# One-hot table rows on two engines, rows loaded on a second queue, states copied by ScalarE, and a gate in four pieces

## The chip, the core and the metric

One core of a Trainium2 chip runs the whole program. The metric is the device time of one execution in microseconds (us). The engines are named as in the profile: PE (TensorE, matrix products), PEld (its weight loads), DVE (VectorE), ACT (ScalarE), POOL (GpSimd) and SP (SyncE, which issues most DMAs).

## The reference

The input x has 8 batches of 512 tokens of 512 values. A layer norm gives xn, from which two branches are computed, and the result joins them:

```python
xn = layernorm(x)
s  = attention(xn)          # q, k silu'd and rotated; linear attention in chunks of 128 with decay;
                            # 16 heads of 32; gated by sigmoid(xn @ Wg1 @ Wg2); rmsnorm by head; @ Wo
g  = silu(mixture(xn))      # router: top 4 of 16 experts, softmaxed; each expert silu(x@wg)*(x@wu)@wd,
                            # plus a shared expert with a sigmoid gate
out = x + s * g
```

In a chunk the attention makes the scores k q times a decay mask, and a state (32 x 32 for each head) is carried from chunk to chunk: S_new = lam_C * S + k v.

## The kernel before

The program is one straight trace for a planner, which orders the instructions of DVE, ACT, POOL and SP by its own costs and due times; the order of PE is that of the trace (`on_pe`), and `behind(engine)` pins single instructions of other engines. The stages follow each other:

1. **First pass (0 to about 208 us).** For each batch b: `norm` (statistics on DVE, the root on POOL), `halves` (16-bit copies on POOL), `turn` (PE transposes), `route_1`, `route_2` (top 4) and `share_1`, `share_2` (shared expert). `load_x(b)` (L142 to L148) loads a batch into one of three buffers; a buffer is free when the transposes, the copies and the store of its old batch are done. These pieces are interleaved with the attention of batch 0, `sequence(0)`. Groups g of four heads go through `key`, `query` (`rotated`, L594: four projection steps on PE, Silu on ACT, then DVE's shuffle, two products and a sum), `by_token` (L618: transposes into bank "k", then kd on DVE), `scores` (L634) and `output` (L675).
2. **Sorting (about 208 to 250 us).** `sort` computes for each token and choice its place in a list of 143 blocks of 128 rows, by expert.
3. **Table (250 to 325 us), beside `sequence(1)`.** `table` (L463) turns the places into a list of tokens: for each 128 tokens it makes two one-hot matrices, `place` (128 wide, L497, then multiplied by the token's number, L499) and `block` (143 wide, L502), all f16 and from SBUF, and PE adds up place^T block (L516). 64 lists go in 8 groups of 16. The buffers stand in the room of the last `LATE` experts' weights, whose loads wait for the table's end. `table` is a generator: `between[0]()` takes one piece of it after each projection step on PE in `rotated` and `value`. A group is four pieces: `make` for the next group, then 5, 5 and 6 matmuls. `sequence(1)` has 8 projections of four steps, 32 pieces.
4. **Blocks (about 340 to 800 us).** For each of 143 blocks: a gather (POOL's queue), a DMA transpose of half of the row (SP's queue), PE transposes of the other half (`transpose_x`), copies on ACT (`join`), `gate_up` (L1042), Silu on ACT (L1046), `transpose_h`, `down`. `gate_3(FIRST)`, the Sigmoid gate of batch 2, stands behind the gate_up of block 2.
5. **The remaining attention (about 800 us to the end).** `sequence(b)` for b = 2 to 7, with the mixture's gathers and sums (`mixture`, `last`) on POOL, DVE and ACT beside it.

PSUM banks have tags: four "a", one "k", one "m", two "d". The four score banks ps (L654), the table's pn (L512), the gate's p2 (L585) and the blocks' transposes all take "a" in turn. In `scores`, DVE reads the states' products straight from bank "k" (L657, L659), makes qd (L664), and then reads the four score banks (L670); `by_token` of the next group writes bank "k" again. `sequence` calls `gate_3(b)` after the first key when batch b has no gate yet, which is so for b = 1.

Of the kernel before, what the change touches and what calls it, by code (L numbers as in the profile page):

```python
# [10 lines left out]
F32 = mybir.dt.float32  # L11
# [8 lines left out]
P = 128  # L20
# [74 lines left out]
def tile_block(ctx: ExitStack, tc: tile.TileContext, a: dict, out: bass.AP):  # L95
# [8 lines left out]
    def bank(tag, name):  # L104
        return pp.tile([P, 512], F32, tag=tag, name=name, bufs={"a": 4, "k": 1, "m": 1, "d": 2}[tag])
# [34 lines left out]

    xs_of = {}

    def load_x(b):
        t = p1.tile([P, NC, D], F32, tag="x", name=f"x_{b}", bufs=3)
        rows = x[b].rearrange("(t p) d -> p t d", p=P)
        for ts in [slice(i, i + 1) for i in range(NC)] if b == 0 else [slice(0, NC)]:
            nc.sync.dma_start(t[:, ts, :], rows[:, ts, :])
        xs_of[b] = t  # L148

    load_x(0)  # L150
    ident = load(const, "ident", [P, P])
    rt_w = load(p1, "rt_w", [P, KC, Q])
    fold = load(p1, "fold", [P, EA])
    load_x(1)
# [308 lines left out]
    def table(room):  # L463

        acc = room[:, :NB]
        free = [2 * NB + 2]
        half = room.bitcast(F16)
        quads = GROUP // QUAD  # L470

        def part(*shape):
            n = int(np.prod(shape))
            free[0] += n
            flat = half[:, free[0] - n : free[0]]
            return flat.rearrange("p (q j) -> p q j", j=QUAD) if len(shape) == 2 else (
                flat.rearrange("p (u q j) -> p u q j", u=quads, j=QUAD))

        count = part(NB, QUAD)
        nc.scalar.copy(count, whole.unsqueeze(2).to_broadcast([P, NB, QUAD]))  # L480
        homes = [(part(quads, P, QUAD), part(quads, NB, QUAD)) for _ in range(2)]

        def rows(of, n):
            return of.rearrange("p (u j) -> p u j", j=QUAD).unsqueeze(2).to_broadcast(
                [P, of.shape[-1] // QUAD, n, QUAD])

        def make(i):
            place, block = homes[i // GROUP % 2]
            for u in range(0, quads, 2):
                us = slice(u, u + 2)  # L490
                lists = slice(i + u * QUAD, i + (u + 2) * QUAD)
                first = lists.start % NT

                def counts(n):
                    return count[:, :n].unsqueeze(1).to_broadcast([P, 2, n, QUAD])

                nc.vector.tensor_tensor(  # L497
                    place[:, us], counts(P), rows(sp[:, 0, lists], P), ALU.is_equal)
                nc.vector.tensor_tensor(  # L499
                    place[:, us], place[:, us], rows(token[:, first : first + 2 * QUAD], P),  # L500
                    ALU.mult)
                nc.vector.tensor_tensor(  # L502
                    block[:, us], counts(NB), rows(sp[:, 1, lists], NB), ALU.is_equal)

        make(0)
        yield
        for i in range(0, TOPK * NT, GROUP):
            if i + GROUP < TOPK * NT:
                make(i + GROUP)
            yield  # L510
            place, block = homes[i // GROUP % 2]
            pn = bank("a", f"pn_{i}")  # L512
            for some in ((0, 5), (5, 10), (10, GROUP)):
                with on_pe():
                    for j in range(*some):
                        nc.tensor.matmul(  # L516
                            pn[:, :NB], lhsT=place[:, j // QUAD, :, j % QUAD],
                            rhs=block[:, j // QUAD, :, j % QUAD], start=(j == 0),
                            stop=(j == GROUP - 1))
                if some[1] == GROUP:  # L520
                    if i:
                        nc.vector.tensor_tensor(acc, acc, pn[:, :NB], ALU.add)
                    else:
                        nc.vector.tensor_copy(acc, pn[:, :NB])
                yield
        t = const.tile([P, NB], I32, tag="slot", name="slot")
        nc.vector.tensor_scalar(t, acc, float(B * N // 2), None, ALU.add)
        slots.append(t)
# [4 lines left out]
    def home(b):  # L533
        return other[0] if other and (b - FIRST) % 2 else att
# [44 lines left out]
        g1_of[b] = att.tile([P, N], F32, tag="tmp", name=f"g2_{b}", bufs=TMP)  # L579
        nc.scalar.copy(g1_of[b], pf)  # L580

    def gate_3(b):
        on_of[b] = home(b).tile([P, G, N], F32, tag="on", name=f"on_{b}", bufs=1)
        g1 = g1_of.pop(b)
        p2s = [bank("a", f"p2_{b}_{g}") for g in range(G)]  # L585
        with on_pe():
            for g in range(G):
                gq = slice(g * Q, (g + 1) * Q)
                nc.tensor.matmul(
                    p2s[g], lhsT=wg2[gq, :], rhs=g1[gq, :], start=True, stop=True)  # L590
        for g in range(G):
            nc.scalar.activation(on_of[b][:, g, :], p2s[g], AF.Sigmoid)

    def rotated(b, g, n, w):  # L594
        ps = bank("m" if n == "k" else "d", f"p{n}_{b}_{g}")
# [38 lines left out]
    def scores(b, g):  # L634
# [19 lines left out]
                    nc.tensor.matmul(  # L654
                        pss[j][:, cs], lhsT=kT[hs, cs], rhs=qT[hs, cs], start=True, stop=True)
        st = scr[0].tile([P, NC - 1, HD], F32, tag="state", name=f"state_{b}_{g}")
        nc.vector.tensor_copy(st[:, 0], pkv[:, :HD])  # L657
        for c in range(1, NC - 1):
            nc.vector.scalar_tensor_tensor(  # L659
                st[:, c], st[:, c - 1], lamc[:, g : g + 1], pkv[:, c * HD : (c + 1) * HD],  # L660
                ALU.mult, ALU.add)
        st_of[g] = st
        qd = scr[0].tile([P, NC - 1, C], F32, tag="qd", name=f"qd_{b}_{g}")
        nc.vector.tensor_tensor(  # L664
            qd, qT[:, C:].rearrange("p (c t) -> p c t", t=C),
            dq[:, g].unsqueeze(1).to_broadcast([P, NC - 1, C]), ALU.mult)
        qd_of[g] = qd
# [239 lines left out]
    def first():  # L907

        for b in range(B):
            route_1(b)  # L910
            yield
            share_1(b)
            yield
            if b + 2 < B:
                norm(b + 2)
            if b + 1 < B:
                halves(b + 1)
                turn(b + 1)
                xs_of.pop(b + 1)
                if b + 4 < B:  # L920
                    load_x(b + 4)
                yield
            route_2(b)
            yield
            share_2(b)
            yield
        next(sorting)
# [4 lines left out]
    norm(1)  # L932
    halves(0)
    xs_of.pop(0)
    load_x(3)
    pieces = first()
    for _ in range(5):
        next(pieces)
# [26 lines left out]
        tc.tile_pool(name="exps", bufs=1, side="right", reuse_waits="tile"))  # L965
    wexp = exps.tile([P, EA - 1, WE], F32, tag="wexp", name="wexp")
    wflat = wexp.rearrange("p e w -> p (e w)")
    LATE = 4
    for e in range(E - LATE):
        nc.sync.dma_start(wexp[:, e, :], a["experts"][:, e, :])  # L970
    filling = table(wflat[:, (E - LATE) * WE :])
# [117 lines left out]
    for i in range(NB + 2):  # L1089
        turn_rows(i + 2)  # L1090
        join(i + 1)
        gate_up(i)
        if i == 2:
            gate_3(FIRST)
        transpose_x(i + 2)
        transpose_h(i - 1)
        down(i - 2)
        gather(i + 4)
# [162 lines left out]
```

## Time and profile before

| | us |
|---|---|
| median of 11 runs | 1228.71 (1224.1 to 1233.45) |
| profiled execution | 1230.39 |
| its span | 1228.6 |
| PE busy in the span | 1177.2 (96%) |
| DVE busy | 767.4 (62%) |
| ACT busy | 407.0 (33%) |
| POOL busy | 448.1 (36%) |

The profile shows one execution. "Busy" counts the time of compute instructions; an instruction on DVE, ACT or POOL that waits inside for a port is counted as busy. In a timeline row stand the start, the duration, the engine, the line, the operation, out <- in with shape and number, and in brackets the idle time before it on its engine with what ended it. Neighbouring rows of one engine can overlap by some 0.1 us, so the step from start to start is shorter than the duration.

### The profile page before, as it was taken

How to read it: one execution, taken by the hardware profiler on the slowest of the kernel's cores; microseconds unless marked ns; L12 is line 12 of the kernel's file. 1: busy time of each engine (PE TensorE's matmuls, PEld its weight loads, DVE VectorE, ACT ScalarE, POOL GpSimd, SP SyncE). 2: the span in 40 equal slices, each digit the busy share in tenths (PEclk: the TensorE clock that was granted, in tenths of full speed). 3: DMA queues.
4: the chain of work that ended last, by engine and by line, in shares of the span. 5: the costliest groups of instructions: out<-in, count | busy, mean ns of one | idle time of the engine just before them, and what ended most of it. 6: DMA issues, size and time to landing. Idle time of an engine off the chain costs nothing. (4 is left out here: it accounts for less than half of the span.)

```text
span 1228.6 us, 21563 instructions
## 1 busy us (share of the span) xinstructions
PE 1177.2 (96%) x7799; PEld 698.4 (57%) x7799; DVE 767.4 (62%) x1652; ACT 407.0 (33%) x782; POOL 448.1 (36%) x430
## 2 busy tenths in 40 slices
PE   6998999989999999999999999999999999999997
PEld 3444554446467777777777776544554544445453
DVE  6378554899224444344444444887969789698784
ACT  3343333320254444444443443123141321411420
POOL 3222102100213333333333331580886857848211
PEclk9998999999999999999999999999999999999999
DMA  9784331181459999899998997950845636535011
GB/s 322 259 287 163 117 137 70 26 321 40 170 138 224 233 229 222 224 229 229 228 230 217 228 227 190 327 167 13 284 141 170 214 104 221 167 112 149 24 36 68
DMA packets 167719, 219.77 MB, mean 179 GB/s; under 512 B 93696, under 2 KB 102656, under 8 KB 165696
## 3 DMA queue, kind: packets, MB, share of 16 engines
q1 hardware_dynamic: 145936, 146.17, 40.1%
q0 software_dynamic: 21680, 72.23, 21.0%
q8 instruction: 64, 1.05, 0.4%
q14 instruction: 39, 0.32, 0.1%
HBM read 127.25 MB, written 72.35 MB: 162 GB/s over the span
## 5 line engine op out<-in xcount | busy, mean ns | idle before, releaser
L1042 PE MATMUL pgu<-wexp,xt 128*128 x1144 | 271.5, 381 | 2.6 <-ACT xt L1023 2.4
L1042 PEld LDWEIGHTS pgu<-wexp,xt 128*128 128x128 f32 x1144 | 217.3, 191 | 94.4 <-issue 31.4
L1001 POOL DMA_INDIRECT xg<-xn_d,slot x83 | 78.7, 948 | 284.2 <-DVE y L1072 168.2
L1047 DVE TENSOR_TENSOR slb<-slb,pgu 128x128 f32<-128x128 f32 x143 | 41.2, 288 | 206.1 <-ACT slb L1046 206.1
L1121 POOL DMA_INDIRECT yg<-y_d,posi x128 | 142.3, 1112 | 50.3 <-DMA m<-sh_d 22.7
L1025 ACT COPY xt<-pl 128x512 uint16<-128x512 uint16 x143 | 109.7, 767 | 149.2 <-DMA pl<-xg 91.5
L1063 PE MATMUL py<-wexp,hT 128*128 x286 | 147.3, 597 | 0.0
L556 PE MATMUL pv<-wv,xT 128*128 128x512 f32 x256 | 121.0, 611 | 4.3 <-DVE sh L370 2.6
L598 PE MATMUL pk<-xT,wk 128*128 128x512 f32 x256 | 120.9, 612 | 0.0
L598 PE MATMUL pq<-xT,wq 128*128 128x512 f32 x256 | 115.9, 593 | 0.0
L731 PE MATMUL pw<-wo,on 128*128 128x512 f32 x224 | 100.9, 596 | 1.5 <-ACT so L904 0.7
L1001 POOL DMA_INDIRECT more<-xn_d,slot x60 | 56.7, 945 | 114.4 <-DVE y L1072 113.5
L1153 POOL TENSOR_TENSOR xo<-xo,m 128x512 f32<-128x512 f32 x30 | 43.8, 1460 | 146.9 <-DVE m L1149 138.6
L1072 DVE TENSOR_SCALAR y<-py,xg 128x512 f32<-128x512 f32 x83 | 62.2, 750 | 30.2 <-PE py L1063 30.2
L556 PEld LDWEIGHTS pv<-wv,xT 128*128 128x128 f32 x256 | 46.5, 193 | 60.9 <-issue 55.2
L670 DVE TENSOR_TENSOR sc<-ps,dmask 128x512 f32<-128x512 f32 x128 | 79.4, 683 | 1.0 <-PE ps L654 1.0
L598 PEld LDWEIGHTS pq<-xT,wq 128*128 128x128 f32 x256 | 47.4, 191 | 52.1 <-issue 50.9
L598 PEld LDWEIGHTS pk<-xT,wk 128*128 128x128 f32 x256 | 46.7, 193 | 49.4 <-issue 47.1
L1046 ACT ACTIVATE slb<-pgu 128x128 f32<-128x128 f32 x143 | 39.7, 278 | 95.8 <-PE pgu L1042 95.2
L731 PEld LDWEIGHTS pw<-wo,on 128*128 128x128 f32 x224 | 41.3, 190 | 51.3 <-issue 44.7
L603 ACT ACTIVATE sk<-pk 128x512 f32<-128x512 f32 x32 | 19.1, 596 | 117.5 <-PE pk L598 102.1
L1072 DVE TENSOR_SCALAR y<-py,more 128x512 f32<-128x512 f32 x60 | 45.0, 750 | 20.6 <-PE py L1063 20.6
(166 smaller groups left out, 1749.5 us busy)
## 6 DMA issues: line engine op xcount, KB each, us to landing
y_d<-y SPq DMA_DIRECT2D x143, 256.0 KB, 2.9
wexp<-in_experts SPq DMA_DIRECT2D x16, 768.0 KB, 10.8
sh_d<-sh SPq DMA_DIRECT2D x32, 256.0 KB, 2.6
m<-sh_d SPq DMA_DIRECT2D x32, 256.0 KB, 4.1
xo<-in_x SPq DMA_DIRECT2D x32, 256.0 KB, 3.7
out<-xo SPq DMA_DIRECT2D x32, 256.0 KB, 2.3
x<-in_x SPq DMA_DIRECT2D x7, 1024.0 KB, 7.1
xT_d<-xT SPq DMA_DIRECT2D x7, 1024.0 KB, 5.1
```

The source lines that it names most:

```text
L556: nc.tensor.matmul(pv, lhsT=xT_of[b][:, k, t * P : (t + 1) * P], rhs=wv[:, k, :], start=(k == 0), stop=(k == KC - 1))
L598: nc.tensor.matmul(ps, lhsT=w[:, k, g * P : (g + 1) * P], rhs=xT_of[b][:, k, :], start=(k == 0), stop=(k == KC - 1))
L670: nc.vector.tensor_tensor(s, pss[j].rearrange("p (c t) -> p c t", t=C), dmask[:, g * HG + j].unsqueeze(1).to_broadcast([P, NC, C]), ALU.mult)
L731: nc.tensor.matmul(pw, lhsT=on_of[b][:, g, t * P : (t + 1) * P], rhs=wo[:, g, :], start=(g == 0), stop=(g == G - 1))
L1001: nc.gpsimd.indirect_dma_start(out=row(i), out_offset=None, in_=xn_d, in_offset=bass.IndirectOffsetOnAxis(ap=slot[:, i : i + 1], axis=0))
L1025: nc.scalar.copy(xt[:, KP:, :].bitcast(U16).rearrange("p k (t h) -> p h k t", h=2), turned(i).rearrange("p (h k) t -> p h k t", h=2))
L1042: nc.tensor.matmul(pg[:, : 2 * F], lhsT=xt[:, k, :], rhs=wflat[:, bass.ds(off + k * 2 * F, 2 * F)], start=(k == 0), stop=(k == KC - 1))
L1047: nc.vector.tensor_tensor(sl, sl, pg[:, F : 2 * F], ALU.mult)
L1063: nc.tensor.matmul(py, lhsT=hT_of.pop(i), rhs=wflat[:, bass.ds(off_of.pop(i) + KC * 2 * F, D)], start=True, stop=True)
L1072: gone.append(nc.vector.tensor_scalar(y, py, row(i).bitcast(F32)[:, bass.ds(at, 1)], None, ALU.mult).ins)
L1121: nc.gpsimd.indirect_dma_start(out=yg, out_offset=None, in_=y_d, in_offset=bass.IndirectOffsetOnAxis(ap=posi[:, r, g : g + 1], axis=0))
L1153: nc.gpsimd.tensor_tensor(xo, xo, m, ALU.add)
```

## The change

- `load_x` takes a queue. Batches 3 to 7 are loaded on POOL's queue, not SP's. `ident` is loaded between the first and the second piece of x_0.
- `table` has three pairs of buffers in place of two, so that it takes the room of five late experts (`LATE = 5`). The multiplication by the token's number runs on POOL. Groups 0 and 1 are made at the start, then five pieces are empty; after that a piece is 5, 5 or 6 matmuls, and `make` for the group after the next stands ahead of the first of the three.
- In `scores`, ACT copies all three states' products from bank "k" into SBUF, and DVE's two steps read them there. The first copy on DVE (L657) is gone. For b < 2, qd is made on POOL.
- `gate_3` takes a list of groups. For batch 2 its four groups stand behind gate_up of blocks 2, 3, 4 and 5, one in each.

```diff
-    def load_x(b):
+    def load_x(b, queue=nc.sync):
...
-            nc.sync.dma_start(t[:, ts, :], rows[:, ts, :])
+            queue.dma_start(t[:, ts, :], rows[:, ts, :])
+            if b == 0 and ts.start == 0:
+                xs_of["ident"] = load(const, "ident", [P, P])
...
-    ident = load(const, "ident", [P, P])
+    ident = xs_of.pop("ident")
...
-        homes = [(part(quads, P, QUAD), part(quads, NB, QUAD)) for _ in range(2)]
+        homes = [(part(quads, P, QUAD), part(quads, NB, QUAD)) for _ in range(3)]
...
-            place, block = homes[i // GROUP % 2]
+            place, block = homes[i // GROUP % 3]
...
-                nc.vector.tensor_tensor(
+                nc.gpsimd.tensor_tensor(
                     place[:, us], place[:, us], rows(token[:, first : first + 2 * QUAD], P),
                     ALU.mult)
...
         make(0)
-        yield
+        make(GROUP)
+        for _ in range(KC + 1):
+            yield
         for i in range(0, TOPK * NT, GROUP):
-            if i + GROUP < TOPK * NT:
-                make(i + GROUP)
-            yield
-            place, block = homes[i // GROUP % 2]
+            if i + 2 * GROUP < TOPK * NT:
+                make(i + 2 * GROUP)
+            place, block = homes[i // GROUP % 3]
...
-    def gate_3(b):
-        on_of[b] = home(b).tile([P, G, N], F32, tag="on", name=f"on_{b}", bufs=1)
-        g1 = g1_of.pop(b)
-        p2s = [bank("a", f"p2_{b}_{g}") for g in range(G)]
+    def gate_3(b, groups=range(G)):
+        if 0 in groups:
+            on_of[b] = home(b).tile([P, G, N], F32, tag="on", name=f"on_{b}", bufs=1)
+        g1 = g1_of[b]
+        p2s = {g: bank("a", f"p2_{b}_{g}") for g in groups}
...
-        nc.vector.tensor_copy(st[:, 0], pkv[:, :HD])
+        nc.scalar.copy(st.rearrange("p c e -> p (c e)"), pkv[:, : (NC - 1) * HD])
         for c in range(1, NC - 1):
             nc.vector.scalar_tensor_tensor(
-                st[:, c], st[:, c - 1], lamc[:, g : g + 1], pkv[:, c * HD : (c + 1) * HD],
-                ALU.mult, ALU.add)
+                st[:, c], st[:, c - 1], lamc[:, g : g + 1], st[:, c], ALU.mult, ALU.add)
...
-        nc.vector.tensor_tensor(
+        (nc.gpsimd if b < FIRST else nc.vector).tensor_tensor(
             qd, qT[:, C:].rearrange("p (c t) -> p c t", t=C),
             dq[:, g].unsqueeze(1).to_broadcast([P, NC - 1, C]), ALU.mult)
...
-                    load_x(b + 4)
+                    load_x(b + 4, nc.gpsimd)
...
-    load_x(3)
+    load_x(3, nc.gpsimd)
...
-    LATE = 4
+    LATE = 5
...
-        if i == 2:
-            gate_3(FIRST)
+        if 2 <= i < 2 + G:
+            gate_3(FIRST, [i - 2])
```

More of the change, by code (lines that the diff above doesn't have):

```diff
@@ L580, in gate_2 @@
         nc.scalar.copy(g1_of[b], pf)
-    def gate_3(b):
-        on_of[b] = home(b).tile([P, G, N], F32, tag="on", name=f"on_{b}", bufs=1)
-        g1 = g1_of.pop(b)
-        p2s = [bank("a", f"p2_{b}_{g}") for g in range(G)]
+    def gate_3(b, groups=range(G)):
[3 more added lines that the diff above has]
+        p2s = {g: bank("a", f"p2_{b}_{g}") for g in groups}
         with on_pe():
-            for g in range(G):
+            for g in groups:
                 gq = slice(g * Q, (g + 1) * Q)
@@ L590, in gate_3 @@
                     p2s[g], lhsT=wg2[gq, :], rhs=g1[gq, :], start=True, stop=True)
-        for g in range(G):
+        for g in groups:
             nc.scalar.activation(on_of[b][:, g, :], p2s[g], AF.Sigmoid)
+        if G - 1 in groups:
+            g1_of.pop(b)
     def rotated(b, g, n, w):
```

## The prediction

> **What bounds the kernel now.** I read the page's shares first, then the waits with TensorE (PE) as the waiting engine, then the stretches by time, then the timeline around the longest waits. The chain view names only the closing addition (L1159), so it says nothing of the middle. The page:
>
> ```profile
> PE 1177.2 (96%) x7799; PEld 698.4 (57%) x7799; DVE 767.4 (62%) x1652; ACT 407.0 (33%) x782; POOL 448.1 (36%) x430
> ```
>
> PE is idle for only 51.4 of 1228.6 us, so a change that takes no PE work away can gain only from idle pieces that it removes. About 19 us of them lie at the two ends (10.3 in the first 30 us, 8.6 in the last 29). The waits that this change aims at:
>
> ```profile
> PE pn L516 <- DVE sc L670: 6.4, 3, 4.3
> PE pk L625 <- DVE state L659: 4.1, 4, 1.6
> PE pt L1016 <- ACT on L592: 1.9, 1, 1.9
> ```
>
> Columns: us in total, times, longest. Together 12.4 us, plus some clock loss behind the longest. The stretches of the table (core time, then PE, PEld, DVE, ACT, POOL busy, granted clock):
>
> ```profile
> 250.00:270.00 20.00, 15.73 (x111) 8.31 (x110) 18.02 (x34) 5.51 (x9) 0.00 (x0) 0.91 0.96 364
> 270.00:300.00 30.00, 27.38 (x318) 17.82 (x317) 29.25 (x59) 3.67 (x5) 0.00 (x0) 1.00 0.33 127
> ```
>
> VectorE (DVE) is 90 and 98% busy, GpSimd (POOL) idle, and the clock is 0.91 around the 4.27 us stall: here DVE sets PE's pace. The timeline shows how:
>
> ```profile
> 250.89 0.69 DVE L497 TENSOR_TENSOR wexp<-wexp,sp 128x1024 f16<-128x1024 f16 x1 [1.04 <-ACT wexp L480]
> ...
> 257.51 2.48 DVE L670 TENSOR_TENSOR sc<-ps,dmask 128x512 f32<-128x512 f32 x4
> 258.25 0.82 PE L516 MATMUL pn<-wexp 128*128 128x143 f16 x5 [4.27 <-DVE sc L670]
> ```
>
> From 250.89 DVE builds one-hot rows; only at 257.51 does it read the four score banks (tag "a") that PE needs again.
>
> **Table: the multiplication moves to POOL.** Sixteen L499 instructions leave DVE, each 0.60 us from start to start: 9.6 us of DVE. What they cost on POOL, no row shows. The nearest are additions of 512 f32 on POOL, and a 16-bit copy:
>
> ```profile
> L1127 POOL TENSOR_TENSOR yg<-yg,yg 128x512 f32<-128x512 f32 x32 | 41.4, 1293 | 1.4 <-DMA yg<-y_d,posi 0.9
> L381 POOL TENSOR_TENSOR wr<-oh,w 128x512 f32<-128x512 f32 x3 | 5.1, 1686 | 0.2
> L266 POOL COPY hs<-x 128x512 uint16<-128x512 uint16 x32 | 21.6, 715 | 18.0 <-DMA xn_d<-hs 18.0
> ```
>
> An undisturbed L381 with a broadcast operand took 1.37 us. The new one has 1024 elements. By bytes it is 1.27 us (as a 512 f32 addition), by elements 2 x 1.37 = 2.75. The 16-bit copy spends 0.61 us undisturbed on 512 elements, about 1.2 ns each, which doesn't look like two elements at a time; so I lean to elements, less one fixed part of about 0.2 (the 128x4 L249 takes 0.23): 2 x 1.3 - 0.2 = 2.4 us. (By the Trainium skill, "GPSIMD Engine Reference", Elementwise — side-by-side cycle accounting, a two-input operation costs some 2.6 cycles of 1.2 GHz per element, an estimate of 2.2 us and a start for 1024; no row here shows it for f16.)
>
> What decides is what POOL does to DVE meanwhile. Later in the same trace both work:
>
> ```profile
> 865.12 2.16 DVE L1149 TENSOR_TENSOR m<-m,s 128x512 f32<-128x512 f32 x1
> ...
> 877.38 2.14 DVE L607 TENSOR_TENSOR qT<-sq,cos 128x512 f32<-128x512 f32 x1
> 877.69 1.27 POOL L1127 TENSOR_TENSOR yg<-yg,yg 128x512 f32<-128x512 f32 x1
> ```
>
> A DVE operation with both inputs in SBUF takes 0.68 us alone, but 2.14 here: it ends 0.56 us after POOL's addition does. A POOL addition at 874.64 that met a running DVE operation took 1.64 instead of 1.27, so they take turns. DVE operations that read PSUM (L692, L670) keep 0.68 and 0.62 under POOL. These rows are f32; the new pairs are f16. (The Trainium skill, "SBUF — State Buffer", Who interferes with whom, states an exclusive lock for a DVE operation with two SBUF inputs against a GpSimd one that reads SBUF, with no exception by type; it speaks against this change: by it the sum below stands, without it the table gains 6 us as in rival two. That no run here shows f16 is why I keep both.)
>
> So I count one shared way to SBUF. Before the last multiplication DVE needs it for 16 place rows x 0.60, 16 block rows x 0.66 and 12 rotation steps (L607 to L609 of two keys and two queries) x 0.60 = 27.4 us; POOL for 16 x 2.4 = 38.4, three qd (moved to POOL for b < 2; 384 elements, about 1.0 each) and 16 gaps of 0.15: 43.8. Sum 71.2 us, from 250.9 to 322.1. Of PE's order there then remains: half of the last group and a projection step 2.2, output(1,3), gate_1 and squares 5.0 (before: 313.54 to 318.50), value(2,3) 3.5. That puts L719 at 332.8; before it began at 324.23: **+8.6 us**.
>
> The other bound is PE's own path. All of make(0) and make(16) now stand before the attention's DVE work: 8 operations, 5.0 us, with three multiplications of 2.4 between them, and the state steps, which now read only SBUF, behind the fourth: scores are read from about 265.7, first bank free at 266.3. PE, done with key(1,2) at about 255.6, waits there at gate_3(1), some 10.7 us. Before, gate_3 began at 263.56 with 2.6 us of pn work behind it, that is like 261.0, so PE is 5.3 us later, less the other two L516 waits (0.95 + 1.21): +3.1. The later bound holds. I take **+9**, for some idle between turns. Ends: at 2.75 us each the port sum grows by 5.6 (+14); at 1.27 it ends at 304 and doesn't bind, and PE's path gives 266.3 - 4 x 1.13 = 261.8, that is +0.8 - 2.2 = -1.4. POOL's queue there holds nothing else than qd; output(1,g) on PE waits for that.
>
> **Gate spread over blocks 2 to 5.** The rows:
>
> ```profile
> 348.33 1.14 PE L589 MATMUL p<-g,wg 32*128 32x512 f32 x8
> ...
> 349.38 1.28 ACT L592 ACT_TABLE_LOAD   x1
> 350.68 2.06 ACT L592 ACTIVATE on<-p 128x512 f32<-128x512 f32 x4
> 351.33 0.69 PE L1016 MATMUL pt<-ident,more 128*128 128x128 f32 x2 [1.85 <-ACT on L592]
> ```
>
> Eight matmul instructions end in 1.14 us, as long as two take alone (L578, 1.13): four row groups run at once. Spread, each goes alone, 2 x 0.436 (L731: 24 in 10.46) = 0.87, four 3.5 us, so PE gains 2.4 us of work. And Silu (L1046) stands between the Sigmoids, with its own 1.28 us load at 353.02: eight loads for two. ACT per block: 0.28 + 0.77 + 0.37 for the block and 2 x 1.28 + 0.55 = 4.5 us, against a block of 2.92 (gate_up starts 360.08 and 363.00) + 0.87 = 3.8. Short by 0.7 x 4 = 2.9, less a lead of about 1.7 (ACT's idle before L1046): 1.2 of stall. Sum 3.5 + 1.2 against 1.14 + 1.85: **+1.7**. Ends: lead hides all, +0.5 (0 if a slow block behind the old stall, 0.46, goes too); hides nothing, +3.4. (The Trainium skill, "ScalarE: Activation LUTs", What ACT_TABLE_LOAD costs, adds a drain of 1.38 us to each switch, which would make it some 8 us more; here the Sigmoid starts 1.30 us after its load does, so the row decides.)
>
> **State by ACT.** The copy frees bank "k" before DVE's chain, so up to 4.1 us of L625 waits go. The new wait: the copy is queued on ACT behind the mixture's Silu, which waited 72.7 us in 19 pieces (longest 8.6) for DVE; by_token on PE waits for it, with one projection (3.5 us) as cover. DVE loses 32 copies of 0.18, but its steps now take turns with POOL. Between -4.1 and +5 (one wait of 8.6 past its cover); nearer the first, as ACT is only a third busy: **-2**.
>
> **No net time.** Loads of x on POOL's queue: five issues of about 1 us (L1121, 1.1; SP's took 0.4), waiting for turn(b+1); behind each stands the next rstd, before which POOL was idle 5.7 us or more from 57 us on. One such load costs DVE a wait of 1.62 us at 108.75, and with it part of a 3.37 us PE wait at 113.83: between -1.6 and +2. ident one issue earlier frees PE at 5.9 instead of 6.44, but PE then waits for sw at 13.55 all the same, and sw keeps its place: 0 to -0.5. Four qd on POOL in sequence(0): cover is its idle time. One expert more after the table: 768 KB, about 3 us at 235 GB/s, beside projections that need none of it; +2 if the first gathers wait.
>
> **Sum.** 9 + 1.7 - 2 = +8.7 us. The profiled execution took 1230.39 (span 1228.6 and 1.8 around it), 1.7 above the median 1228.71 of 11 runs; against its own time that is 1239.1, on the median's footing 1237.4; I forecast 1237.
>
> **Rivals.** Likeliest (0.6): one port, elements; 1231 to 1249. Rival one (0.15): POOL handles f16 by bytes; -1.4 + 1.7 - 2 = -1.7, 1227. For it: f16 doubles DVE's rate (1024 in 0.69); against it: the 16-bit copy. Rival two (0.2), on the other side: f16 one-hot rows on DVE don't take turns with POOL, whatever POOL takes up to 3 us. Then DVE's 5.0 us of makes stand alone, the first bank is free at 256.8, PE is 4.2 earlier than 261.0, and 2.2 of later waits go: -6.4 + 1.7 - 2 = -6.7, 1222. It decides once place and block keep 0.69 beside L499. Against it: every f32 pair seen. Rival three (0.05): ACT's queue blocks the state copies as well, +5 more than -2: above 1244, up to 1255.
>
> **Numbers.** 0.3% (3.7 us) is about what a measurement of this kernel can tell from no change: 1225.0 to 1232.4. Faster: rival two and part of rival one, 0.23. Same: the rest of it and the lower edge of the first, 0.14. Slower: 0.63. Range 1221 to 1249; the likeliest case's own is 1231 to 1249.
>
> **What would show it.** Right: L499 on POOL at 2.2 to 2.8 us; L497 and L502 with means well above 0.75; a PE wait at L589 or L516 of several us before 270; L719 after 330; nine L592 and L1046 table loads in place of three around 343 to 365; L625 waits under 1 us. Wrong: L497 at 0.69 beside POOL, L589 of group 1 by 258, L719 before 322.

## The result, and the profile after

The changed kernel takes 1259.11 us (median of 8 runs, 1255.64 to 1263.72), the kernel before beside it 1227.66: ratio 1.0254, 95% interval 1.0236 to 1.0272, so 31 us slower. Forecast were 1237 us and a range up to 1249: the sign was right, the size was not. The profiled execution took 1256.39 us, with a span of 1254.6.

I cut both spans at the same events: the copy of the count tile by ACT, the first pb matmul behind the table, the first Silu of an expert block, the last one, and the span's end.

| stretch | before, us | after, us | difference |
|---|---|---|---|
| start to count copy | 249.9 | 250.9 | +1.0 |
| count copy to pb (the table's stage) | 74.3 | 94.5 | +20.2 |
| pb to first block | 20.5 | 19.3 | -1.2 |
| first to last block | 420.7 | 416.8 | -3.9 |
| last block to the square roots of sequences 2 and 3 | 66.9 + 75.7 | 71.7 + 78.7 | +7.8 |
| from there to the end | 320.6 | 322.7 | +2.1 |

The two executions profiled differ by 26.0 us, the medians by 31.5. The blocks' -3.9 us says little: over the twenty profiles of this document that stretch took 416.1 to 423.1 us, and 416.9 to 420.1 in kernels whose table is as fast as before. Start with the page's shares: PE's busy time grew by 9.2 us for the same 7799 matmuls; a slower clock is in that.

```profile
PE 1186.4 (95%) x7799; PEld 703.6 (56%) x7799; DVE 786.3 (63%) x1596; ACT 424.0 (34%) x820; POOL 498.7 (40%) x459
```

The stretches of the table's stage (core time; PE, PEld, DVE, ACT, POOL busy; granted clock):

```profile
250.00:270.00 20.00, 8.72 (x74) 4.76 (x73) 18.92 (x21) 3.71 (x6) 13.73 (x6) 0.78 0.90 349
270.00:300.00 30.00, 26.36 (x199) 16.43 (x195) 21.99 (x34) 5.11 (x8) 12.52 (x6) 0.80 0.18 75
300.00:330.00 30.00, 24.58 (x299) 16.25 (x298) 22.66 (x38) 2.25 (x5) 14.23 (x7) 0.94 0.18 63
```

Before, the clock was 0.91, then 1.00 and 1.00. Over the whole stage, from the count copy to pb, PE was busy for 65.4 us before and 73.4 after; what these 8.0 us are follows below. The waits of PE over the whole span, in total, times, longest:

```profile
PE p L593 <- DVE sc L675: 11.3, 1, 11.3
...
PE pw L736 <- DVE m L1154: 5.4, 4, 1.8
PE pg L572 <- DVE sc L675: 4.4, 2, 2.4
PE ps L660 <- DVE sc L675: 4.4, 2, 3.6
...
PE pn L519 <- DVE sc L675: 3.5, 1, 3.5
```

Inside the table's stage PE waits 20.9 us in all, against 8.7 before: +12.2. Three waits are long, all for VectorE's reading of scores. The timeline of VectorE and GpSimd shows why the first is:

```profile
251.88 0.69 DVE L499 TENSOR_TENSOR wexp<-wexp,sp 128x1024 f16<-128x1024 f16 x1 [1.05 <-ACT wexp L482]
252.50 0.75 DVE L504 TENSOR_TENSOR wexp<-wexp,sp 128x1144 f16<-128x1144 f16 x1
253.16 2.38 DVE L499 TENSOR_TENSOR wexp<-wexp,sp 128x1024 f16<-128x1024 f16 x1
...
267.58 2.47 DVE L675 TENSOR_TENSOR sc<-ps,dmask 128x512 f32<-128x512 f32 x4
```

```profile
252.66 2.33 POOL L501 TENSOR_TENSOR wexp<-wexp,token 128x1024 f16<-128x1024 f16 x1 [18.85 <-DVE wexp L499]
255.62 2.34 POOL L501 TENSOR_TENSOR wexp<-wexp,token 128x1024 f16<-128x1024 f16 x1 [0.63 <-DVE wexp L499]
...
267.74 1.89 POOL L501 TENSOR_TENSOR wexp<-wexp,token 128x1024 f16<-128x1024 f16 x1 [0.63 <-DVE wexp L499]
```

The comparison that starts at 253.16 beside a multiplication lasts 2.38 us instead of 0.69, and ends 0.55 us after it: f16 operations take turns like the f32 ones of the trace before. The Trainium skill, "SBUF — State Buffer", Who interferes with whom, says so without exception by type; the row agrees. GpSimd waits too: the multiplication at 252.66 starts while the block row of 252.50 runs and lasts 2.33 us; the one at 267.74 meets only reads of score banks, which lie in PSUM, and lasts 1.89. Its own work is 1.9 us. What a long wait does behind itself, on PE:

```profile
268.31 3.86 PE L593 MATMUL p<-g,wg 32*128 32x512 f32 x8 [11.28 <-DVE sc L675]
...
286.74 2.07 PE L660 MATMUL ps<-qT,kT 32*128 32x128 f32 x8 [3.63 <-DVE sc L675]
288.75 2.08 PE L604 MATMUL pk<-xT,wk 128*128 128x512 f32 x2
...
293.30 1.04 PE L604 MATMUL pk<-xT,wk 128*128 128x512 f32 x2
...
312.00 0.82 PE L519 MATMUL pn<-wexp 128*128 128x143 f16 x5 [3.51 <-DVE sc L675]
312.64 1.97 PE L559 MATMUL pv<-wv,xT 128*128 128x512 f32 x2
```

A pair of projection matmuls takes 2.08 us right behind a wait and 1.04 some 5 us later: each of these waits is paid a second time. The gate's 3.86 us (1.14 at 348.33 of the trace before) is only in part the clock: its matmuls start at 268.31, 268.91, 269.51 and 270.11, as VectorE frees one score bank after the other. The rows that ran slow behind the three waits (the pairs of 1.91, 2.08, 1.42, 1.97 and 1.47 instead of 1.04, the ps row of 2.07 instead of 1.15, and smaller ones) add up to some 6 us by my count, against 1.4 before. So of the 8.0 us more of busy time, some 4.5 are the clock; the rest is matmuls that start bank by bank.

### The profile page after: what moved, and what is told of

It is laid out like the page before. It is cut to its first block, busy times and chain, and to the rows that moved or that the text cites. A ratio compares the mean times of both kernels' runs of the same rounds, so it can differ in the third digit from the quotient of the medians.

```text
span 1254.6 us, 21638 instructions
## 1 busy us (share of the span) xinstructions
PE 1186.4 (95%) x7799; PEld 703.6 (56%) x7799; DVE 786.3 (63%) x1596; ACT 424.0 (34%) x820; POOL 498.7 (40%) x459
## 5 line engine op out<-in xcount | busy, mean ns | idle before, releaser
L501 POOL TENSOR_TENSOR wexp<-wexp,token 128x1024 f16<-128x1024 f16 x16 | 36.7, 2295 | 48.3 <-DVE wexp L499 47.6
```

## The experiments

They ran on several chips; the kernel before took 1245.3, 1245.4, 1228.2, 1227.7 and 1241.2 us beside them. So all are told by the ratio to the kernel before on the same chip; 0.1% is 1.2 us. "Step" is the time from the count copy to the first pb matmul, from the profile.

### The parts one by one

Five kernels each put one part into the kernel before. First the multiplication alone:

```
-                nc.vector.tensor_tensor(
+                nc.gpsimd.tensor_tensor(
                     place[:, us], place[:, us], rows(token[...], P), ALU.mult)
```

> The kernel before with that one line moved to GpSimd. Turns at one way to SBUF: L497's mean goes above 1.1 us, L499 takes 2.2 to 2.4 on GpSimd, and the time is 10 to 25 us above before (1238 to 1253). If the layout of the pieces makes the loss: within 4 us of 1228.

Ratio 1.0087 [1.0057, 1.0117], step 86.9 us. The groups (busy, mean ns, idle before):

```profile
L499 POOL TENSOR_TENSOR wexp<-wexp,token 128x1024 f16<-128x1024 f16 x16 | 35.4, 2215 | 63.9 <-DVE wexp L497 63.9
L497 DVE TENSOR_TENSOR wexp<-wexp,sp 128x1024 f16<-128x1024 f16 x16 | 21.4, 1336 | 3.6 <-PE pn L516 2.5 <-ACT wexp L480 1.0
```

VectorE lost 16 instructions of 0.69 us, and its comparisons for `place` became nearly twice as long. Then the table's new layout with the multiplication on VectorE: three homes, rows two groups ahead, the start five pieces later, no piece for making alone, LATE 5.

```
         make(0)
-        yield
+        make(GROUP)
+        for _ in range(KC + 1):
+            yield
         for i in range(0, TOPK * NT, GROUP):
-            if i + GROUP < TOPK * NT:
-                make(i + GROUP)
-            yield
+            if i + 2 * GROUP < TOPK * NT:
+                make(i + 2 * GROUP)
```

> The kernel before with the table's new layout alone: three buffers, groups 0 and 1 made at the start, two groups ahead, LATE = 5, and the multiplication still on VectorE. If the order costs by itself (the scores' reads queue behind both groups, and gate_3 of batch 1, which needs all four banks, meets that wait), the table's stage is some 7 us longer than before (74.3 us) and the time is 5 to 9 us above before. If GpSimd makes the whole loss and the earlier end of the table is a gain, the time is 0 to 5 us below before.

Ratio 1.0077 [1.0046, 1.0107], step 82.9 us. Nothing in it touches GpSimd, so the new layout was no gain but a loss of its own. The state copied by ACT, alone:

```
-        nc.vector.tensor_copy(st[:, 0], pkv[:, :HD])
+        nc.scalar.copy(st.rearrange("p c e -> p (c e)"), pkv[:, : (NC - 1) * HD])
...
-                st[:, c], st[:, c - 1], lamc[:, g : g + 1], pkv[:, c * HD : (c + 1) * HD],
-                ALU.mult, ALU.add)
+                st[:, c], st[:, c - 1], lamc[:, g : g + 1], st[:, c], ALU.mult, ALU.add)
```

> The kernel before with the states copied by ScalarE, nothing else. The prediction's own value is 2 us below before (the L625 waits of 4.1 us go). The rival from the trace after: the wait only moves from the transposes to the next matmul that needs a score bank, and L659's second SBUF input doubles its mean (0.245 to about 0.5 us), so 0 to 6 us above before.

Ratio 1.0029 [1.0007, 1.0051]. The steps on VectorE now have two inputs in SBUF, and take turns with GpSimd. In the sequence of batch 3, first this kernel, then the one with the gate spread (states as before, same chip):

```profile
891.96 2.27 DVE L659 SCALAR_TENSOR_TENSOR state<-state,lamc 128x32 f32<-128x32 f32 x2
894.89 1.06 PE L569 MATMUL pg<-xT,wg 128*32 128x512 f32 x8 [1.92 <-DVE sc L669]
```

```profile
893.61 0.53 DVE L662 SCALAR_TENSOR_TENSOR state<-state,lamc,pk 128x32 f32<-128x32 f32 x2
894.93 1.06 PE L569 MATMUL pg<-xT,wg 128*32 128x512 f32 x8
```

The two steps take 2.27 us instead of 0.53, the scores behind them are read later, and PE waits. Between the square roots of batches 2 and 3 this kernel takes 80.3 us, the other 76.4. The gate spread, alone:

```
-        if i == 2:
-            gate_3(FIRST)
+        if 2 <= i < 2 + G:
+            gate_3(FIRST, [i - 2])
```

> The kernel before with the gate of batch 2 spread over blocks 2 to 5, nothing else. The prediction's value is 1.7 us above before; by the trace after (block 8 stands 26.0 us behind block 0 in both) it is within 1 us of before.

Ratio 1.0008 [0.9987, 1.003]: nothing measurable. The x loads on GpSimd's queue, with the identity's load moved up behind the first piece of x:

```
-            nc.sync.dma_start(t[:, ts, :], rows[:, ts, :])
+            queue.dma_start(t[:, ts, :], rows[:, ts, :])
+            if b == 0 and ts.start == 0:
+                xs_of["ident"] = load(const, "ident", [P, P])
```

> The kernel before with x of batches 3 to 7 loaded on GpSimd's queue and ident loaded second, nothing else. The prediction's value is no change (between -2 and +2 us). If the part of the loss that lies outside the table's stage (some 9 us of 31) comes from here, 3 to 9 us above before, with the table starting that much later than at 249.9.

Ratio 1.0070 [1.0044, 1.0097]. The five add to 0.87 + 0.77 + 0.29 + 0.08 + 0.70 = 2.71%; the whole change measured 2.54%. The parts account for the whole within their intervals (qd on GpSimd, which has no run of its own, is not among them), and a part forecast at nothing costs a quarter of it.

To separate the loads from the identity I moved the loads alone:

```
-    def load_x(b):
+    def load_x(b, queue=nc.sync):
...
-                    load_x(b + 4)
+                    load_x(b + 4, nc.gpsimd)
...
-    load_x(3)
+    load_x(3, nc.gpsimd)
```

> The kernel before with only the five later loads of x moved to GpSimd's queue; the identity's load stays where it was. Theory (the loads are the whole of the 8.6 us of the run with both): they are issued behind GpSimd's row copies and land later, VectorE waits 11 to 14 us in four pieces for x (1.6 before), the count copy comes at 251 to 252 us (248.3 in kernels with the old loads on this chip), ratio 1.005 to 1.009. Rival (the identity's place in the queue costs): count copy at 248 to 249 us, ratio 0.999 to 1.002.

Ratio 1.0059 [1.0042, 1.0075]; it is the loads. VectorE's waits for x between 40 and 250 us:

```profile
DVE st L245 <- DMA x<-in_x: 11.5, 4, 4.8
```

Before, this line read 1.6, 1, 1.6. GpSimd's part:

```profile
52.82 2.85 POOL L266 COPY hs<-x 128x512 uint16<-128x512 uint16 x4
55.97 0.82 POOL L147 DMA_DIRECT2D x<-in_x  x1 [0.30 <-POOL hs L266]
...
72.89 2.86 POOL L266 COPY hs<-x 128x512 uint16<-128x512 uint16 x4
75.70 0.83 POOL L147 DMA_DIRECT2D x<-in_x  x1
```

Each load stands behind the copies of hs. Yet the issues at 55.97 and 75.70 are not later than SP's were (65.23 and 77.39), so it is not the issue. The data take longer to land: 8.5 us in the median of these five, 7.1 in that of SP's seven. Above all VectorE asks sooner. The planner gave its queue another order: the statistics of batches 3, 5 and 6 begin at 47.12, 64.07 and 84.19, where they began at 54.21, 77.66 and 93.11, and there they wait. The end also grew: from the last square root to the end of the span 84.2 us instead of 82.8, with the last output issued at 1223.57 (1223.46 before) and spans of 1230.0 and 1228.6. All seven profiled kernels with these loads on GpSimd show 84.2 to 84.4 us there. Where the rest of the 7 us goes I did not find; the profiled execution, at 1232.07, is the fastest of this kernel's runs.

### The change with one part undone

The multiplication back on VectorE:

```
-                nc.gpsimd.tensor_tensor(
+                nc.vector.tensor_tensor(
                     place[:, us], place[:, us], rows(token[...], P), ALU.mult)
```

> The changed kernel with the multiplication by the token's number back on VectorE; the rest of the change stays. If GpSimd's multiplications and VectorE's two-input operations take turns at one way to SBUF, the one-hot rows (L499) return from a mean of 1.31 us to 0.69, the wait at L593 falls from 11.3 us to 3 to 4 (twelve operations of 0.6 us ahead of the scores' reads), L724 of batch 1 starts at 324 to 328 in place of 345.4, and the time is 1238 to 1243 us. If instead the new layout of the pieces (two groups ahead) makes the loss, the time stays within 5 us of 1259.

Ratio 1.0181 [1.0131, 1.0231], step 81.5 us: of the table's +20.2, 13.0 belong to GpSimd's turns. The wait fell as foretold, the time did not: 1.0181 is some 1250 us, not 1238 to 1243, as the layout's part stays. The wait before the gate is 3.22 us there, and still the clock is 0.83 from 260 to 300 us. The state's copy and steps back on VectorE:

```
-        nc.scalar.copy(st.rearrange("p c e -> p (c e)"), pkv[:, : (NC - 1) * HD])
+        nc.vector.tensor_copy(st[:, 0], pkv[:, :HD])
...
-                st[:, c], st[:, c - 1], lamc[:, g : g + 1], st[:, c], ALU.mult, ALU.add)
+                st[:, c], st[:, c - 1], lamc[:, g : g + 1], pkv[:, c * HD : (c + 1) * HD],
+                ALU.mult, ALU.add)
```

> The changed kernel with the states read from PSUM by VectorE again. If the two SBUF inputs of L665 cost, by turns with GpSimd, its mean returns from 0.512 to 0.245 us, and of the 8 us that the changed kernel loses in the stretch from the end of the blocks to the second Square root load (781 to 931 us) most come back: 1250 to 1254 us. If that stretch differs by the order that the planner happens to choose, or the stretch isn't bound by VectorE: within 3 us of 1259.

Ratio 1.0286 [1.0234, 1.0338]: no gain in the whole, though the steps fell from 0.51 to 0.24 us. In the stretch between the square roots of batches 2 and 3 the gain is there, 76.5 us against 80.2 and 80.3 in the two other changed kernels of this chip; the table's stage of the profiled execution was 97.8 us, 3.3 longer than in the changed kernel, and I don't know why. Seven us of matmuls whose result nobody reads, ahead of the gate:

```
             if g == 0 and b not in on_of:
+                for w in range(2):
+                    pw = bank("d", f"warm_{w}")
+                    with on_pe():
+                        for k in range(KC):
+                            nc.tensor.matmul(
+                                pw, lhsT=wk[:, k, :P], rhs=xT_of[b][:, k, :],
+                                start=(k == 0), stop=(k == KC - 1))
                 gate_3(b)
```

> The changed kernel with 8 more products of two matmuls (some 7 us of TensorE work into banks that nobody reads) ahead of the gate of batch 1, in the 11.3 us in which TensorE waits there. If the long wait lowers TensorE's clock and the slow matmuls behind it are on the path: the clock between 270 and 300 us goes from 0.80 to over 0.95, and the time falls by 5 to 8 us (1251 to 1254) although work was added. If the stage is bound by VectorE and GpSimd alone and the clock is only a sign of it: within 2 us of 1259.

Ratio 1.0281 [1.0225, 1.0336]. The theory failed: the wait shrank to 4.42 us, but the clock between 270 and 300 us was 0.79, and the next pair took 1.91 us as in the changed kernel. A wait of 4.4 us is left there, and behind it the gate whose matmuls start one bank at a time. That alone can do it: in a kernel further below (two groups ahead, rows held back) the gate waits for only 0.31 us, takes 2.91, and the next pair takes 1.92. So this run does not price the clock.

### Turns, or waiting for GpSimd's results?

In the change VectorE could also be late because it depends on GpSimd. Here sixteen multiplications on a spare tile are added to the kernel before, and nothing reads them:

```
+                nc.gpsimd.tensor_tensor(
+                    spare, spare, rows(token[...], P), ALU.mult)
```

> The kernel before with sixteen more multiplications on GpSimd, of the size of the moved ones, from and into a spare tile that nothing else reads, beside the same rows on VectorE; the multiplications proper stay on VectorE, so nothing waits for GpSimd's results. Theory (f16 operations with two inputs in SBUF take turns between the two engines): the one-hot comparisons beside them grow from 0.69 to a mean of 1.1 to 1.6 us, the step is 84 to 92 us, ratio 1.008 to 1.015. Rival (the lengthening came from waiting for GpSimd's results, not from sharing): comparisons stay at 0.69 to 0.75, step 74 to 76 us, ratio 0.999 to 1.002.

(The spare tile takes the room of a fifth late expert and is cleared once, on GpSimd.) Ratio 1.0200 [1.0183, 1.0216], step 101.6 us, more than foretold: GpSimd waits for nothing here and runs all sixteen back to back from 251.70 to 288.34, so nearly every row ahead of the scores takes its turn, and PE waits 19.11 us for them. The groups of VectorE:

```profile
L506 DVE TENSOR_TENSOR wexp<-wexp,sp 128x1144 f16<-128x1144 f16 x16 | 20.2, 1264 | 0.0
L501 DVE TENSOR_TENSOR wexp<-wexp,token 128x1024 f16<-128x1024 f16 x16 | 18.8, 1175 | 0.0
L499 DVE TENSOR_TENSOR wexp<-wexp,sp 128x1024 f16<-128x1024 f16 x16 | 17.6, 1102 | 3.9 <-PE pn L520 2.9 <-ACT wexp L480 1.0
```

All three kinds, 0.68 to 0.75 before, grow by 0.4 to 0.5 us without depending on GpSimd. The way to SBUF is the cause; 16 free multiplications cost 25 us.

### Why does being ahead cost anything?

My theory was the order on VectorE's queue: rows ahead of scores. Two kernels hold all rows but the first group's behind the scores, with the table's new start and pieces; one is one group ahead, one two (there `make(GROUP)` stands behind the five pieces):

```
+                def late():
+                    return behind(DVE) if i else nullcontext()
...
+                with late():
                     nc.vector.tensor_tensor(
                         place[:, us], counts(P), rows(sp[:, 0, lists], P), ALU.is_equal)
```

> The kernel before, its table on VectorE alone and one group ahead, but only the first group's rows stand ahead of the first scores on VectorE's queue, the other groups' rows are held in program order behind the scores, and the table starts five pieces later. Theory (it is the order on VectorE's queue that costs PE, by the wait and by the lower clock after it): the 4.27 us wait of the pn matmuls for the scores falls under 1 us, the granted clock between 250 and 270 us is over 0.97 (0.91 before), the step from the count copy to the first pb matmul is 66 to 71 us (73.6 to 74.8 in kernels with the table of before), and the time is 4 to 8 us below the kernel before, ratio 0.993 to 0.997. Rival (VectorE's sum of work bounds the stage, so what is held back is only late elsewhere): step 73 to 76 us, ratio 0.999 to 1.002.

> The table two groups ahead with three homes on VectorE alone, as measured before at ratio 1.0077 and a step of 82.9 us, but with only the first group's rows ahead of the first scores and the rest held behind them. Theory (rows that stand ahead of the scores are the cost of being two ahead): step 66 to 72 us, ratio 0.993 to 0.998. Rival (the third home, the fifth expert behind the table or VectorE's sum of work is the cost): step 80 to 84 us, ratio 1.006 to 1.009.

Both were wrong: ratios 1.0068 [1.0055, 1.0081] and 1.0087 [1.0068, 1.0105], steps 86.6 and 87.0. The first wait did fall, to 0.32 and 0.31 us, but others came. The first kernel's PE:

```profile
254.52 2.91 PE L595 MATMUL p<-g,wg 32*128 32x512 f32 x8 [0.32 <-DVE sc L676]
...
272.62 2.07 PE L660 MATMUL ps<-qT,kT 32*128 32x128 f32 x8 [4.03 <-DVE sc L676]
...
297.05 0.81 PE L522 MATMUL pn<-wexp 128*128 128x143 f16 x5 [2.02 <-DVE sc L676]
```

```profile
270.00:300.00 30.00, 23.70 (x196) 15.15 (x197) 23.26 (x48) 1.20 (x2) 0.00 (x0) 0.81 0.26 102
300.00:330.00 30.00, 27.74 (x272) 17.17 (x269) 17.03 (x33) 3.44 (x7) 0.74 (x1) 0.85 0.14 47
```

The rows held back stand ahead of the next scores instead, and the clock is 0.81 and 0.85. That left the pieces. In the diff a `yield` is gone (the table has 128 lists, 8 groups of 16, not the 64 named at the start): a group now has three pieces, all with pn matmuls, where it had four, one only for making rows. A projection has room for four pieces, so it carries four rounds of pn matmuls instead of three, and VectorE must make rows a third faster. Three kernels: the new start and pieces alone, the distance alone, and the holding back alone.

```
         make(0)
-        yield
+        for _ in range(KC + 1):
+            yield
         for i in range(0, TOPK * NT, GROUP):
             if i + GROUP < TOPK * NT:
                 make(i + GROUP)
-            yield
```

> The kernel before with one part of the table's new order alone: the table starts five pieces later and each group has three pieces instead of four, so four pieces of pn matmuls stand in each projection instead of three; rows still on VectorE and one group ahead. Theory (density: six projections instead of eight must carry the table, VectorE falls behind in them and PE waits for scores at each, with the clock lowered after each wait of 2 us or more): step from the count copy to the first pb matmul 83 to 88 us (74.3 before), ratio 1.006 to 1.010. Rival (rows that stand ahead of the scores are the cost): step 73 to 77 us, ratio 0.998 to 1.002.

Ratio 1.0015 [1.0, 1.0031], step 80.9: the pieces cost 6.6 us in the stage, of the theory's kind, though less than its 83 to 88. The time shows only some 1.8 us of it; where the rest goes, one profiled execution doesn't tell.

The distance alone keeps the old start and pieces, with the third home and LATE 5:

```
         make(0)
+        make(GROUP)
         yield
         for i in range(0, TOPK * NT, GROUP):
-            if i + GROUP < TOPK * NT:
-                make(i + GROUP)
+            if i + 2 * GROUP < TOPK * NT:
+                make(i + 2 * GROUP)
             yield
```

> The kernel before with the rows built two groups ahead in three homes, on VectorE, but with the old start and the old four pieces for a group. Theory (density is the cost, not the distance ahead): the first wait for scores grows from 4.3 to 5 to 7 us, later ones shrink, step 74 to 78 us, ratio 0.999 to 1.004. Rival (rows that stand ahead of the scores are the cost): step 80 to 85 us, ratio 1.006 to 1.009.

Ratio 0.9995 [0.9982, 1.0008], step 74.0, with a first wait of 5.23 us: distance alone is free.

The holding back alone is the `late()` of above, with the old start and pieces:

> The kernel before with its old pieces, and only the rows of the later groups held behind the scores on VectorE's queue. Theory: VectorE reads the scores at about 255 us, the first wait of the pn matmuls falls from 4.3 to 1.2 to 2.0 us and no lower clock follows it, step 68 to 72 us, ratio 0.994 to 0.998. Rival (VectorE's sum of work bounds the stage, so the time held back is lost at the next scores): step 73 to 78 us, ratio 0.999 to 1.003.

Ratio 0.9990 [0.9977, 1.0004], step 72.4: the rival was nearer. So on VectorE alone neither pieces nor distance cost much; together they cost 9.5 us. Part of that lies elsewhere: that kernel's VectorE waits 5.87 us before the norm multiplication for something that the trace only calls "remote", and PE 4.07 us for it. I can't say what it was. Three of the changed kernels, all on one other chip, show it at the same place; the like kernel with rows held back, on a third chip, does not, and is as slow (1.0087). Why the two together cost more than their sum stays open. Last, the changed kernel with the old start and pieces:

```
         make(GROUP)
-        for _ in range(KC + 1):
-            yield
+        yield
         for i in range(0, TOPK * NT, GROUP):
             if i + 2 * GROUP < TOPK * NT:
                 make(i + 2 * GROUP)
+            yield
```

> The changed kernel with one thing undone: the table starts where it did before and each group has its old four pieces (three pieces of pn matmuls to a projection); multiplications on GpSimd, three homes, two groups ahead, and all other parts as changed. Theory (the packing of the pieces costs here what it cost on VectorE alone, 10 us between the kernels with 1.0077 and 0.9995): step 84 to 88 us (94.5 in the changed kernel), ratio 1.015 to 1.019. Rival (the turns with GpSimd bind the table whatever the pieces are): step 92 to 96 us, ratio 1.022 to 1.026.

Ratio 1.0259 [1.0213, 1.0306], step 88.9: the stage got 5.6 us shorter, the way to the first block 4.5 longer, and the time did not move. Its first wait:

```profile
269.64 0.82 PE L519 MATMUL pn<-wexp 128*128 128x143 f16 x5 [12.98 <-DVE sc L675]
```

With turns, a round of place and block rows takes 2.96 us (254.49 to 257.45 there), and six place rows stand ahead of the scores whatever the pieces are. By the time the rival held; the step, 88.9, lies between the two forecasts.

### The clock's share

Filling PE's one long wait in the table of before with matmuls that nobody reads:

```
+            if i == 0:
+                warm = bank("d", "warm")
+                with on_pe():
+                    for k in range(8):
+                        nc.tensor.matmul(warm, lhsT=wk[:, k % KC, :P], rhs=wk[:, k % KC, :],
+                                         start=(k == 0), stop=(k == 7))
             pn = bank("a", f"pn_{i}")
```

> The kernel before with eight matmuls of 128x512, whose result nobody reads, placed on PE where it waits 4.3 us for the scores (3.5 us of work in a wait that is there anyway). Theory (a wait of over some 2 us lowers the granted clock for the 5 us after it): the wait shrinks to about 0.8 us, the eight gate matmuls behind it take 1.14 instead of 1.59 us, the clock between 250 and 270 us is 1.00 instead of 0.91, the step is 71 to 72.5 us (74.3), ratio 0.997 to 0.998. Rival (the clock goes its own way, or VectorE decides the end of the stage anyway): step 74 to 75 us, ratio 0.999 to 1.001.

Ratio 1.0009 [0.9993, 1.0025], step 75.2. I had mis-sized the filler: the profile counts eight such f32 matmuls as 16, and they took 7.03 us, not 3.5, so it overshot the 4.27 us wait. The stretch:

```profile
250.00:270.00 20.00, 20.00 (x121) 10.31 (x120) 17.40 (x34) 5.59 (x9) 0.00 (x0) 1.00 0.94 363
```

The clock stayed at 1.00. Counted from VectorE's first row the first pn matmul comes 2.46 us later than before (9.82 instead of 7.36); but from there to the gate PE takes 3.91 us instead of 5.31. So the lower clock had cost 1.4 us behind this wait. The gate itself took 1.59 us at full clock too; that part of the theory was wrong. Then the kernel that holds rows back, changed so that only half of the first group's rows stand before the first score and the other half behind it:

```
-        make(0)
+        make(0, [0])
+        second.append(lambda: make(0, [2]))
         yield
...
             sc_of[g].append(s)
+            if second:
+                second.pop()()
```

> The kernel before with its old pieces, and on VectorE only the first three row operations ahead of the first score; the other three of the first group stand between the first score and the second, all later rows behind the scores. Theory (the first wait and the lower clock behind it are the whole excess of this stage): no wait over 1 us at the first pn matmuls, clock 1.00 between 250 and 270 us, step 68 to 71 us (74.3 before), ratio 0.995 to 0.998. Rival (VectorE's sum of work bounds the stage): the wait turns up at the next scores or rows, step 72 to 75 us, ratio 0.999 to 1.001.

Ratio 0.9991 [0.9964, 1.0018], step 72.7. The first wait is 0.16 us; then PE waits 1.47 us for VectorE's copy of the first pn, behind rows and scores, and is slow again (clock 0.91 between 250 and 270 us, not 1.00). From 270 to 300 us VectorE is busy for 29.48 of 30 us: so what is left of the stage looks like its work, not its order. No kernel here beats the one before by more than its interval.

## Why the prediction was right in sign and wrong in size

**Turns: right; the port's sum: right by luck.** "One shared way to SBUF" held for f16. A multiplication took 2.30 us in the mean (2.4 forecast), but 1.89 where it met no row of VectorE's: the term was 0.5 us too large, sixteen times. The sum also let the way never stand idle, and it did: from 273.7 to 276.7, for one, both engines wait for PE or for each other. The two errors cancel, and the last multiplication ended at 321.55 (322.1 forecast). Rivals one (1.27 us) and two fell with it, and so did rival three: the table's long waits are for scores, and the longest for ACT is 1.89 us, before the gate at 844.78.

**Table, +9: mis-sized; +20.2 at pb.** The sum of the port met its mark, but it was not the later bound. The step that failed is PE's own path: "so PE is 5.3 us later, less the other two L516 waits (0.95 + 1.21): +3.1". The first wait was sized well (10.7 us to 266.3; measured 11.28 to 268.31), though for four rounds of rows, and two place rows of the third group stand ahead of the scores as well. But the other waits did not go; they became 3.63 and 3.51 us. I had let one bank's first wait stand for the stage, though VectorE was as late at every score. And the clock after a wait had no term at all, while the trace of before showed one (0.91, and a pair at 1.69 instead of 1.04). Waits are +12.2 us, the clock some 4.5, and matmuls that start bank by bank the rest. That the removed `yield` packs the table was not priced either; alone it costs 6.6 us in the stage, and some 1.8 in the time.

**Gate, +1.7: nothing measurable (1.0008).** The interval of the time alone would allow +1.7; the trace doesn't. From the first to the ninth block the span is 26.05 us before and 26.04 after. Before, the single gate made one block interval 7.74 us (348.44 to 356.18) instead of 2.92, a stall of 4.8 and not the 3.0 that I had counted; after, four intervals of 4.42 and a short one of 1.70 come in its place. The loads were as foretold: nine between 363 and 385.

**State, -2: +3.6 (1.0029).** The L625 waits did go. But PE's next matmul needs a bank of scores, and VectorE was late with those too:

```profile
826.64 1.07 PE L572 MATMUL pg<-xT,wg 128*32 128x512 f32 x8 [1.99 <-DVE sc L675]
827.63 5.40 PE L559 MATMUL pv<-wv,xT 128*128 128x512 f32 x8
```

What was freed came due one step later, and here with it the clock: the value projection takes 5.40 instead of 3.70. The step that failed is named in the prediction and not priced: "its steps now take turns with POOL". Two steps ahead of the scores took 2.27 us instead of 0.53. I asked where the wait goes for ACT's queue only, not for the next bank.

**Loads, "No net time": +7 to +9.** The bound "between -1.6 and +2" came from the one existing wait; four waits of 11.8 us in sum appeared in the changed kernel. That the planner would order VectorE's queue anew, and ask for x up to 13.6 us sooner, was not thought of. A step called free needs its cover checked for the data's arrival, and for the order that the planner then makes.

**What would show it wrong** named L719 before 322; it began at 345.4, far past the "after 330" of the right side. The range left no room above because the table's and the loads' terms had a bound from one event each.

## What to carry to other kernels

Before moving an elementwise operation to GpSimd, count what VectorE does beside it with two inputs in SBUF: each waits for the whole of GpSimd's instruction, and 16 multiplications of 1.9 us cost 11 us though GpSimd had nothing else to do. Price a new PE wait of 2 us or more with a slow stretch behind it (likely from 2 us, in these profiles certain from 3.5), and ask at every later bank whether the engine that was late once is late again. Removing a wait on an engine whose neighbour is 98% busy moves the wait; it pays only if that neighbour has less to do.

## What the runs showed of the hardware

- Every PE wait of 3.5 us or more was followed by some 4 to 6 us in which 128x512 f32 matmuls took up to 2.1 us a pair instead of 1.04. Shorter ones did it in some cases: of twenty waits between 2.0 and 2.9 us, counted over all profiles from 31 us on, thirteen did and seven did not (2.44 us at 910.42 of the changed kernel, 2.88 at 311.88 of the one with the old pieces). 1.47, 1.68 and 1.86 us did, 1.46 and 1.67 did not. The Trainium skill, "TensorE: Matmul & The Clock Gate", Why this matters for your kernels, warns of gaps over some 3 us; here less was enough in part of the cases.
- Turns do not depend on data: an unrelated f16 multiplication on GpSimd lengthened the f16 row of VectorE's that met it from 0.69 to 2.38 us, as the real one did.
- Loads of 1 MB on GpSimd's queue came with 1.4 us more at the end of the program, long after the last of them.
